# The last chunk's outer column sums on VectorE, and the last but one chunk's store from SyncE

## The chip, the cores and the metric

The kernel runs on one core of one Trainium2 chip, as a single launch. The metric is device time in microseconds. A core has five engines with an in-order instruction queue each: TensorE (PE; its weight loads are listed as PEld), VectorE (DVE), ScalarE (ACT), GpSimd (POOL) and SyncE (SP). DMAs can be issued from several of them; here SP issues plain DMAs, and GpSimd issues plain ones and those that add what they read to what is at the destination (accumulating DMAs). An instruction that waits on a semaphore holds everything behind it on its own queue.

## The reference

The input is four images of 256 channels and 56 x 56 points, in f32. Four layers follow, each of the form x + layer(group_norm(x)) with 32 groups:

```python
# layer 0 and 2: involution, a 7x7 kernel computed per point (16 groups of 16 channels)
h    = einsum('bchw,oc->bohw', x, reduce_w)      # 256 -> 64; layer 2: batch norm, relu
kern = einsum('bchw,oc->bohw', h, span_w)        # 64 -> 49 * 16
out  = (kern * patches(x)).sum(over the 49 taps) # layer 2: batch norm, relu
# layer 1: two 3x3 convolutions over 256 channels
h = relu(bn(conv3x3(x, w1)))
h = bn(conv3x3(h, w2))
out = relu(x + h)
# layer 3: gates from 2-d Fourier transforms of the image
out = x * sigmoid(real fft mean @ W.T + b) + x * spatial_factor
```

The change lies in layer 1, in its second convolution. Here `x` inside the layer is the normalized input, so that the result of the layer is xin + relu(xnorm + bn(conv(h))), where xin is the input before the norm.

## The kernel before

`involution_layer` does layer 0, `conv_layer` layer 1, and `involution_layer` again layers 2 and 3. Images that aren't in SBUF lie in DRAM, in one tensor for each layer, image and half of the channels (128 of 256).

**Tiling of the convolution.** The layer has twelve chunks (`n_chunks = 3 * B`): each image is cut into three bands of rows (`C2_ROWS`: 16, 20 and 20 rows). For each chunk there is a `conv1` and a `conv2`, in the order conv1(i), conv2(i - 1); at the end come conv1(11), conv2(10), conv2(11). So conv2(11), "the last chunk", follows conv2(10), "the last but one", with no conv1 between. Along a row the convolution is done by a transform of six positions for four outputs: `transform` (L1439 to 1455) makes six transformed inputs `v`, TensorE multiplies each with transformed weights, and VectorE combines the six products into four outputs.

**Six positions in order.** `KS = (1, 2, 3, 4, 0, 5)`. In conv2, positions 1, 2, 3 and 5 are `unfiltered` (L1525): three rows of weights for two halves of input channels, with 280 columns. Positions 4 and 0 are filtered (`filtered_product`, L1540): the rows are transformed as well, and the product needs sums and differences of neighbouring rows of `v`. `inner_columns` (L1491 and L1492) makes two of them on VectorE. `outer_columns` makes the other two, v of a row minus v two rows below, in one of two ways:

```python
if (conv, i) == (1, 1):
    tt(t[:, at], v[:, at], v[:, below], ALU.subtract)        # L1505, VectorE
else:
    nc.scalar.mul(t[:, at], v[:, below], -1.0)               # L1507, ScalarE
    nc.gpsimd.dma_start(t[:, at], v[:, at], accum_op=ALU.add)  # L1508, GpSimd
```

Here `tt` is VectorE's tensor_tensor. For the last chunk the destination `t` is free room in the weights of the first convolution (`u1_sb`; the profile shows it as u_sb). A filtered product runs its 16 inner matmuls first and its 16 outer matmuls behind them. ScalarE copies the first inner result (L1549), VectorE makes sum and difference with the second (L1550, L1551), and adds the outer results (L1553). The combination of outputs follows (L1723 to L1734), and after the product of position 5, one half of the output channels at a time (`co` 0 and 1), L1741 and L1742.

**The end of a chunk.** For the last two chunks the residual comes in by `load_residual` (L1392, issued by SP) into one of two buffers that alternate (`new_xr`), and ScalarE scales it (`residual`, L1633). In `joined`, VectorE adds the result of the convolution (L1670). The last chunk then takes VectorE (L1675) and a store from SP (L1676). The last but one uses `added`: a Relu on ScalarE (L1684), an accumulating DMA on GpSimd that adds xin (L1685), and a store on GpSimd (L1686). Its statistics for the next layer's norm are taken on VectorE from the same buffer (`stats`, L1704), in the course of conv2(11). The residual of the last chunk is loaded into the same two buffers, so each load waits for the store and the statistics of the half that it replaces.

**Order of the work.** The order on each engine is the order in which the program calls are made (`in_order`). Twelve lists `after[0]` to `after[11]` hold steps that are run at two points of each of six positions: in `conv2`, `after[2 * n_s]` comes between the two halves of a product (in a filtered product, between L1551 and L1553) and `after[2 * n_s + 1]` behind the combination. For conv2(11): `inner_columns` and the outer sums of position 4 are in `after[2]`, those of position 0 in `after[3]`; the statistics of chunk 10 are in `after[3]` and `after[4]` (co 0) and `after[6]` and `after[7]` (co 1), and the residual loads behind them in `after[4]` and `after[7]`. `added` goes through the list `late_x`: for co 0 it is run at once, for co 1 it is left for `after[0]` of the next piece of work (L1804), that is, for conv2(11) behind the first half of its first product.

Of the kernel before, what the change touches and what calls it, by code (L numbers as in the profile page):

```python
# [73 lines left out]
def net_kernel(  # L74
# [19 lines left out]
    nc = tc.nc  # L94
# [1089 lines left out]
    def conv_layer(xin, xout, st, ahead):  # L1184
        with ExitStack() as es:
# [40 lines left out]
            def new_xr():  # L1226
                n_xr[0] += 1
                at = (n_xr[0] - 1) % 2 * NX
                return room["xr"][:, at : at + NX]
# [9 lines left out]
            def new_outer():  # L1239

                n_v2[1] += 1
                at = (n_v2[1] - 1) % 5
                return room["v2"][:, at * NY : (at + 1) * NY]
# [136 lines left out]
            n_chunks = 3 * B  # L1380
# [86 lines left out]
            def input2(i):  # L1467
                v = v_of[2, i] = v_sb[i == n_chunks - 1]
                p0, p1 = C2_ROWS[i % 3 - 1]
                yield from transform(  # L1470
                    v, ph2, i % 2 * PH_ROWS, (19, 20, 19)[i % 3], v_of.get((2, i - 1)), p1 - p0, known_rows(i, 3)
                )

            def rows_of(conv, i):

                y0, y1 = (C1_ROWS if conv == 1 else C2_ROWS)[i % 3]
                return y1 - y0
# [16 lines left out]
            def outer_columns(conv, i, k):  # L1494

                n = rows_of(conv, i)
                v = v_of[conv, i][:, VP[k]].rearrange("p r t -> p (r t)")
                if (conv, i) == (2, n_chunks - 1):
                    t = u1_sb[:, FILTERED2.index(k)].rearrange("p y k n -> p (y k n)")[:, 2 * NX : 2 * NX + NY]
                else:  # L1500
                    t = new_outer()
                at = slice(0, n * NB * WT)
                below = slice(2 * NB * WT, (n + 2) * NB * WT)
                if (conv, i) == (1, 1):
                    tt(t[:, at], v[:, at], v[:, below], ALU.subtract)  # L1505
                else:
                    nc.scalar.mul(t[:, at], v[:, below], -1.0)  # L1507
                    nc.gpsimd.dma_start(t[:, at], v[:, at], accum_op=ALU.add)  # L1508
                t = t.rearrange("p (r e n) -> p e r n", e=2, n=NB * WT)
                v2_of[conv, i, k, 1] = [t[:, e] for e in range(2)]  # L1510


            def run_all(items):
                while items:
                    items.pop(0)()
# [97 lines left out]
            def conv2(i, after, sums, tail):  # L1613
# [4 lines left out]
                bb = i // 3  # L1618
# [22 lines left out]
                def joined(co):  # L1641

                    y = room["h"][:, : 4 * NY].rearrange("p (j n) -> p j n", j=4)[:, :, co * m : (co + 1) * m]
                    if summed:
                        x, at = new_xr(), slice(y0 * W, y1 * W)
                        xr_of[i, co] = x
                        x = x[:, : n * W]
                        s, t = (raw[:, co : co + 1] for raw in raw_of[bb])
                        by = rstd[:, co : co + 1]

                        def leaves():
                            nc.scalar.activation(x.rearrange("p (q j) -> p j q", j=4), y, AF.Identity, bias=t, scale=s)
                            nc.gpsimd.dma_start(x, xin[bb][co][:, at], accum_op=ALU.add)

                        if co == 0:
                            leaves()
                        else:
                            late_r[0].append(leaves)
                        k = 5 + 2 * co
                        late_r[k].append(lambda: nc.scalar.activation(x, x, AF.Relu, scale=by))  # L1660
                        late_r[k + 1].append(lambda: nc.gpsimd.dma_start(x, xin[bb][co][:, at], accum_op=ALU.add))
                        k = 10 + 2 * co
                        late_r[k + 1].append(lambda: nc.sync.dma_start(xout[bb][co][:, at], x))
                        if bb < B - 1:
                            st = sums[co][:, i % 3]
                            late_r[k].append(lambda: mean_of(st, x))
                            late_r[k + 4].append(lambda: spread_of(st, x))
                        return
                    rj = results[co].rearrange("p (j q) -> p j q", j=4)
                    stt(rj, y, s2_6[:, co : co + 1], rj, ALU.mult, ALU.add)  # L1670
                    x = xr_of[i, co][:, : n * W]
                    xj = x.rearrange("p (q j) -> p j q", j=4)
                    at = slice(y0 * W, y1 * W)
                    if i == n_chunks - 1:
                        stt(xj, rj, 0.0, xj, ALU.max, ALU.add)  # L1675
                        nc.sync.dma_start(xout[bb][co][:, at], x)  # L1676
                    else:
                        late_x.append(lambda: added(x, xj, rj, co, at))
                        if co == 0:
                            run_all(late_x)  # L1680

                def added(x, xj, rj, co, at):

                    nc.scalar.activation(xj, rj, AF.Relu)  # L1684
                    nc.gpsimd.dma_start(x, xin[bb][co][:, at], accum_op=ALU.add)  # L1685
                    nc.gpsimd.dma_start(xout[bb][co][:, at], x)  # L1686

                def mean_of(st, x):

                    nc.gpsimd.memset(st[:, 0:1], float(n * W))  # L1690
                    nc.scalar.activation(x, x, AF.Identity, accum_out=st[:, 1:2])
                    nc.scalar.mul(st[:, 1:2], st[:, 1:2], 1.0 / (n * W))

                def spread_of(st, x):

                    c = small.tile([P, 1], F32, name="c")
                    nc.scalar.mul(c, st[:, 1:2], -1.0)
                    nc.scalar.activation(x, x, AF.Square, bias=c, accum_out=st[:, 2:3])
# [38 lines left out]
                for co in range(NB):  # L1737
                    at = slice(co * m, (co + 1) * m)
                    ps = one_bank()[:, :m]
                    unfiltered(ps, u2_sb, v, 5, co, n)  # L1740
                    stt(q[:, at], q[:, at], -3.0, ps, ALU.mult, ALU.add)  # L1741
                    stt(q[:, at], t[:, at], 4.0, q[:, at], ALU.mult, ALU.add)  # L1742
                    joined(co)
                    run_all(after[10 + co])
# [8 lines left out]
            def columns_at(after, inner, outer, conv, i):  # L1753
                for at, ks in zip(inner, ((1, 2), (3, 4))):
                    after[at].append(lambda ks=ks: inner_columns(conv, i, *ks))
                for at, k in outer:
                    after[at].append(lambda k=k: outer_columns(conv, i, k))
# [6 lines left out]
            for i in range(1, n_chunks):  # L1764
                order += [(1, i), (2, i - 1)]
            order.append((2, n_chunks - 1))
            late_v, late_x, late_r = None, [], [[] for _ in range(24)]
            sums_of = {}


# [27 lines left out]
            for s, (conv, i) in enumerate(order):  # L1798
                after = [[] for _ in range(12)]
# [1 line left out]
                    after[5].append(step(g))  # L1801
                    after[11].append(step(g))
                nxt = order[s + 1] if s + 1 < len(order) else None
                after[0] += late_x  # L1804
                late_x.clear()
                for items in after:
                    items += late_r.pop(0)
                    late_r.append([])
                if conv == 1:
# [3 lines left out]
                    if i > 0:  # L1813
                        after[0].append(lambda i=i: (inner_columns(1, i, 0, 5), outer_columns(1, i, 0)))
                        if i > 1:
                            after[2].append(lambda i=i: outer_columns(1, i, 5))
                    if nxt[0] == 2:
                        j = nxt[1]
                        late_v = input2(j)
# [25 lines left out]
                else:  # L1845
# [10 lines left out]
                    if late_v is not None:  # L1856
                        place(after, late_v, (0, 0, 1, 1))
                        late_v = None
# [44 lines left out]
    def begin_last():  # L1903
# [3 lines left out]
        norm_weights(2, 0)  # L1907

    pending = conv_layer(src[1], src[2], st, begin_last)
    involution_layer(2, src[2], src[3], red2, span2, sb2, blocks, pending=pending)  # L1910

# [64 lines left out]
```

## Time and profile before

| | us |
|---|---|
| median of three runs | 1714.48 |
| the three runs | 1714.85, 1708.15, 1714.48 |
| the profiled execution | 1717.23 |
| its span, first to last instruction | 1715.5 |
| TensorE busy (share of the span) | 1632.9 (95%) |
| VectorE busy | 1333.8 (78%) |
| ScalarE busy | 1000.9 (58%) |
| GpSimd busy | 498.2 (29%) |
| mean granted TensorE clock | 0.979 |

Times in the profile count from the start of the span. In it, conv2(10) ends near 1126 us and conv2(11) near 1173 us. A line of the timeline or of the chain gives the start, the length, and the engine with its line in the code; outputs stand left of the arrow, inputs right. In brackets is the time for which the engine was idle before, and what released it. A wait of an instruction for several semaphores is put down to the one that came last.

### The profile page before, as it was taken

The page shows a single profiled execution, that of the slowest core. Times are in us where ns is not written, and L with a number is a line of the kernel's source. Part 1 is how long each engine was busy: PE and PEld are TensorE (multiplying, and loading weights), DVE is VectorE, ACT ScalarE, POOL GpSimd, SP SyncE. Part 2 cuts the span into 40 slices and gives each one's busy share as a digit, 9 for nine tenths or more (in the row PEclk, how much of TensorE's full clock was granted, in tenths as well). Part 3 has the DMA queues.
Part 4 walks back from the last instruction along what each step waited for, and adds up shares of the span by engine and source line. Part 5 has one row for each costly group of instructions (what it writes and reads, how often), then busy time and mean ns, then how long its engine had stood idle before and what let it go on. Part 6 is the DMA issues. An engine that isn't in the chain of part 4 may idle for free.

```text
span 1715.5 us, 57009 instructions
## 1 busy us (share of the span) xinstructions
PE 1632.9 (95%) x24488; PEld 1466.1 (85%) x24488; DVE 1333.8 (78%) x2439; ACT 1000.9 (58%) x2192; POOL 498.2 (29%) x711
## 2 busy tenths in 40 slices
PE   6999999999989999999999999988999999899988
PEld 4998998988987889899999889976988888788876
DVE  2687787777759998999889899947777778778775
ACT  1655556456545565565666456435667567577654
POOL 2124223322433222212212212110000572572571
PEclk9999999999999999999999999999999999999996
DMA  2354445433759666566766556644444765764762
GB/s 90 114 184 138 147 147 185 154 127 104 238 139 281 112 129 106 121 129 138 148 132 113 109 122 128 142 132 147 129 139 162 207 215 184 218 210 140 204 169 98
DMA packets 92490, 258.63 MB, mean 151 GB/s; under 512 B 14837, under 2 KB 37374, under 8 KB 88526
## 3 DMA queue, kind: packets, MB, share of 16 engines
q1 hardware_dynamic: 57438, 163.33, 29.9%
q0 software_dynamic: 33760, 90.37, 24.8%
q8 instruction: 194, 3.18, 0.8%
q10 hardware_dynamic: 1040, 1.26, 0.3%
q14 instruction: 58, 0.48, 0.1%
HBM read 95.07 MB, written 49.15 MB: 84 GB/s over the span
## 4 chain that ended last, share of the span: by engine, by line
PE 64%; DVE 15%; DMA 7%; issue 5%; ACT 3%; SPq 2%; POOL 2%; ACTq 0%; POOLq 0%; DVEq 0%
PE mm L1540 17%; PE ps L594 15%; PE ps L636 13%; PE mm L1525 11%; DVE kt L612 5%; DMA xw<-xw 4%; PE ps L408 3%; DVE un L656 3%; DMA u_sb<-in_wc_dram 2%; PE ps L470 1%; SPq L426 1%; SPq L427 1%; DVE st L1106 1%; ACT hp L489 1%; ACT xw L420 1%
## 5 line engine op out<-in xcount | busy, mean ns | idle before, releaser
L636 PE MATMUL ps<-kt,xw 126*32 126x48 f32 (+1 forms) x12544 | 381.7, 236 | 24.1 <-DMA xw<-xw 11.3
L636 PEld LDWEIGHTS ps<-kt,xw 126*32 126x32 f32 (+1 forms) x12544 | 343.0, 122 | 69.7 <-issue 44.0
L594 PE MATMUL ps<-hp,z_sb 64*126 64x133 f32 x6144 | 384.3, 279 | 9.0 <-DVE kt L612 4.9
L594 PEld LDWEIGHTS ps<-hp,z_sb 64*126 64x126 f32 x6144 | 364.4, 185 | 25.0 <-DVE kt L612 6.9
L612 DVE TENSOR_TENSOR kt<-ps,zb_sb 126x798 f32<-126x798 f32 x352 | 332.9, 980 | 59.3 <-PE ps L594 47.9
L605 ACT ACTIVATE kt<-ps,zb_sb 126x133 f32<-126x133 f32 x960 | 281.0, 442 | 107.3 <-PE ps L594 107.3
L1525 PE MATMUL mm<-v,u_sb 128*128 128x280 f32 (+2 forms) x1320 | 295.1, 383 | 1.7 <-DVE xs L1551 1.0
L1525 PEld LDWEIGHTS mm<-v,u_sb 128*128 128x128 f32 x1320 | 247.5, 189 | 41.8 <-issue 1.6
L1540 PE MATMUL mm<-xs,u_sb 128*128 128x126 f32 (+2 forms) x1392 | 175.9, 279 | 0.3 <-DVE xs L1551 0.3
L656 DVE SCALAR_TENSOR_TENSOR un<-ps,s,un 128x240 f32<-128x240 f32 x224 | 102.5, 457 | 89.0 <-ACT un L651 83.7
L1540 PEld LDWEIGHTS mm<-xs,u_sb 128*128 128x128 f32 x1392 | 168.5, 193 | 0.5 <-issue 0.5
L656 DVE SCALAR_TENSOR_TENSOR un<-ps,par_sb,un 128x240 f32<-128x240 f32 x224 | 97.6, 456 | 81.8 <-ACT un L649 77.9
L1508 POOL DMA_DIRECT2D xs<-v x82 | 75.2, 1006 | 285.3 <-ACT xs L1507 233.9
L661 POOL TENSOR_TENSOR xs<-un,xs 128x240 f32<-128x240 f32 x112 | 72.2, 665 | 216.3 <-DVE un L656 216.3
L420 ACT COPY xw<-ps 126x896 f32<-126x896 f32 x112 | 101.4, 906 | 39.0 <-PE ps L408 21.3
L649 ACT ACTIVATE un<-ps,par_sb 128x240 f32<-128x240 f32 x112 | 50.3, 449 | 119.1 <-PE ps L636 112.8
L151 POOL TENSOR_TENSOR norm_sb<-norm_sb,mhalf 128x1 f32<-128x1 f32 x32 | 19.8, 642 | 342.5 <-DVE norm_sb L150 342.5
L651 ACT ACTIVATE un<-ps,bn_t,s 128x240 f32<-128x240 f32 x112 | 60.1, 538 | 94.2 <-PE ps L636 86.0
L408 PE MATMUL ps<-ident_sb,strip_sb 128*126 128x128 f32 x784 | 110.6, 281 | 3.9 <-ACT hp L489 1.6
L408 PEld LDWEIGHTS ps<-ident_sb,strip_sb 128*126 128x126 f32 x784 | 84.0, 141 | 15.0 <-POOL strip_sb L393 4.6
L1411 ACT ACTIVATE ph<-xs,norm_sb 128x266 f32<-128x266 f32 (+2 forms) x96 | 80.4, 862 | 9.0 <-DMA xs<-x 7.3
L1540 PE MATMUL mm<-v_sb,u_sb 128*128 128x140 f32 (+2 forms) x536 | 73.5, 280 | 3.5 <-DVE xs L1553 3.0
(303 smaller groups left out, 2272.7 us busy)
## 6 DMA issues: line engine op xcount, KB each, us to landing
xw<-xw SPq DMA_DIRECT2D x224, 252.0 KB
xw<-xw SPq DMA_DIRECT2D x224, 126.0 KB
xs<-x POOLq DMA_DIRECT2D x26, 560.0 KB, 5.9
x<-xs POOLq DMA_DIRECT2D x8, 1568.0 KB, 7.8
xs<-x SPq DMA_DIRECT2D x8, 1568.0 KB
xs<-v POOLq DMA_DIRECT2D x42, 252.0 KB, 4.3
xs<-in_x_dram SPq DMA_DIRECT2D x6, 1568.0 KB
x<-xs SPq DMA_DIRECT2D x6, 1568.0 KB
```

The source lines that it names most:

```text
L408: nc.tensor.transpose(ps[:Q, k * P : (k + 1) * P], flat[:, k * Q : (k + 1) * Q], ident_sb)
L420: nc.scalar.copy(xw[:, :NSB, :], ps[:Q, : NSB * P].rearrange("q (n c) -> q n c", n=NSB))
L594: nc.tensor.matmul(ps[:Q, i, k * NT : (k + 1) * NT], z_sb[i * R : (i + 1) * R, cb * GB // 2 + gp, z0 : z0 + Q], hp[i * R : (i + 1) * R, py ...
L605: nc.scalar.activation(kt[:, g0 + i, pb, :, k], ps[:Q, i, k * NT : (k + 1) * NT], AF.Identity, bias=zb_sb[:, cb * GB + g0 + i, p0 + k : p0 ...
L612: nc.vector.tensor_tensor(kt[:, g0 : g0 + 2, pb], ps[:Q, :, : PB * NT].rearrange("q i (k t) -> q i t k", k=PB), zb_sb[:, cb * GB + g0 : cb ...
L636: nc.tensor.matmul(v[m * j : m * j + m, i, :, k * TP : (k + 1) * TP], xw[:, window(ty), m * j : m * j + m], kt[:, ng * j : ng * j + ng, :, ...
L656: nc.vector.scalar_tensor_tensor(part, o[e], s, part, ALU.mult, ALU.add)
L661: nc.gpsimd.tensor_tensor(dst, u, dst, ALU.add)
L1411: nc.scalar.activation(dst, xr[:, j], AF.Identity, bias=t, scale=s)
L1508: nc.gpsimd.dma_start(t[:, at], v[:, at], accum_op=ALU.add)
L1525: nc.tensor.matmul(ps, *position(u, v, ci, dy, k, co, n), start=(j == 0), stop=(j == NB * 3 - 1))
L1540: nc.tensor.matmul(ps[:, bank, co * m : (co + 1) * m], u[ci][:, co * P : (co + 1) * P], v2[:, : n // 2, ci * WT : (ci + 1) * WT], start=(c ...
```

## The change

There are two edits. The outer column sums of conv2's last chunk are made by one VectorE subtraction for each of positions 4 and 0, where ScalarE's multiply and GpSimd's accumulating DMA made them. In the last but one chunk `added` is called for both halves of the output channels directly in `joined`, without `late_x`, and its store is issued by SP where GpSimd issued it. The Relu and the accumulating DMA stay where they were, on ScalarE and GpSimd.

```diff
@@ outer_columns
-                if (conv, i) == (1, 1):
+                if (conv, i) in ((1, 1), (2, n_chunks - 1)):
                     tt(t[:, at], v[:, at], v[:, below], ALU.subtract)
                 else:
                     nc.scalar.mul(t[:, at], v[:, below], -1.0)
@@ joined
                     else:
-                        late_x.append(lambda: added(x, xj, rj, co, at))
-                        if co == 0:
-                            run_all(late_x)
+                        added(x, xj, rj, co, at)
 
                 def added(x, xj, rj, co, at):
 
                     nc.scalar.activation(xj, rj, AF.Relu)
                     nc.gpsimd.dma_start(x, xin[bb][co][:, at], accum_op=ALU.add)
-                    nc.gpsimd.dma_start(xout[bb][co][:, at], x)
+                    nc.sync.dma_start(xout[bb][co][:, at], x)
@@ conv_layer
-            late_v, late_x, late_r = None, [], [[] for _ in range(24)]
+            late_v, late_r = None, [[] for _ in range(24)]
@@ the loop over the order
-                after[0] += late_x
-                late_x.clear()
```

## The prediction

> **What bounds the kernel now.** I read the page, then the timeline at the end of the convolution layer (1100 to 1180 us), where both edits lie, then the waits, the chain and the stretches there. The page's TensorE is 95% busy over a span of 1715.5 us, so a gain has to come from a place where TensorE stands still. The waits of 1100 to 1180 us (who waited for whom: total us, times, longest) show one:
>
> ```profile
> PE mm L1540 <- DMA u_sb<-v: 7.6, 1, 7.6
> DVE xs L1553 <- PE mm L1540: 8.5, 1, 8.5
> POOL x L1686 <- DMA xs<-x: 11.5, 2, 6.2
> ACT u_sb L1633 <- DMA xs<-x: 18.4, 3, 9.4
> ```
>
> TensorE stops for 7.6 us for the outer column sums of the last chunk (u_sb), and VectorE then stops 8.5 us for TensorE. The chain (start us, us, what) says why the sums are late:
>
> ```profile
> 1140.04 0.86 POOL xs L1685
> 1140.90 6.22 issue
> 1147.12 0.04 POOLq L1508
> 1147.16 0.50 POOL x L1686
> 1147.66 0.01 issue
> 1147.67 4.11 DMA u_sb<-v
> 1151.78 0.14 issue
> 1151.91 4.09 PE mm L1540 x16
> ```
>
> GpSimd issues the residual's accumulation for the second channel half of chunk 10 (L1685), then stands 6.22 us before the store of the same half (L1686), which needs it landed, and only then issues the two accumulations that make the outer sums (L1508). Those land 4.1 us later. The timeline (start, us, engine and line; in brackets the idle time before and its releaser):
>
> ```profile
> 1133.34 0.88 POOL L1685 DMA_DIRECT2D xs<-x  x1 [28.17 <-ACT xs L1684]
> 1135.44 1.22 ACT L1507 ACTIVATE u_sb<-v 128x560 f32<-128x560 f32 x2
> 1136.85 0.74 DVE L1723 TENSOR_TENSOR hp<-hp,mm 128x560 f32<-128x560 f32 x1 [3.25 <-ACT u_sb L1507]
> 1144.79 0.45 DVE L1550 TENSOR_TENSOR xs<-xs,mm 128x280 f32<-128x280 f32 x1 [4.04 <-ACT xs L1549]
> 1148.28 2.36 ACT L1633 ACTIVATE u_sb<-xs,shift,norm_sb 128x1120 f32<-128x1120 f32 x1 [3.52 <-DMA xs<-x]
> 1156.02 0.74 DVE L1553 TENSOR_TENSOR xs<-xs,mm 128x560 f32<-128x560 f32 x1 [8.53 <-PE mm L1540]
> ```
>
> ScalarE's half of the sums was done by 1136.7; eleven more us went by at GpSimd. From 1156.02 VectorE works almost without a gap to the end of the layer (L1675 at 1172.70), and the next layer begins behind it. Here VectorE's chain sets the time, and what releases L1553 is the lever.
>
> **What the Trainium skill says.** "DMA: Bandwidth & Descriptors", section "SWDGE vs HWDGE vs iDMA": an accumulating DMA must come from GpSimd, a plain one may come from SP. So the stores can move and L1685 cannot; the trace has it on GpSimd. Same page, "Queues, rings and completion order": each DMA engine takes turns between queue rows, so a store from SP shares the engines with GpSimd's accumulation in place of standing ahead of it. The load of 1142.65, beside an accumulation, landed after 5.6 us; that of 1160.5, alone, after 3.75. "VectorE: DVE Perf Modes", "The perf-mode tier table": tensor_tensor in f32 runs at one element a cycle; the trace's 560 columns take 0.734 us (L1505, five of them). "TensorE: Matmul & The Clock Gate", Part 1: a window of about 3.4 us idle halves the clock; the trace grants 0.50 from 1152 to 1156, after the stall.
>
> **The change, part by part.**
>
> *Outer sums on VectorE.* Gone: two ScalarE multiplies (2 x 0.655) and two GpSimd DMAs with 4.1 us to landing. Added: two subtractions, 2 x 0.734 = 1.47 us on VectorE. The first follows L1492 at 1133.6, and VectorE then idles to 1136.85 (3.25 us): hidden. The second follows the first statistics of chunk 10 (after 1139.4) and has the 4.04 us ahead of L1550 at 1144.79: hidden too. Without that cover they would cost 1.47. Both are ready ahead of their products, so TensorE goes on at 1144.33 and ends the 16 outer products at about 1146.4 (2.07 us, as the same group at 1113.45), in place of 1155.98 (4.07 at the low clock).
>
> *Store by SP, second half at once.* ScalarE's order stays: the two Relus of L1684 already run back to back, since nothing of ScalarE lies between. On GpSimd, L1685 of the second half waits no more for the first half's landing (1139.4) and store: it is issued when its Relu ends, at 1135.1, 4.9 us earlier. The first accumulation keeps the engines busy from about 1134.9 to 1138.5 (3.7 us; seen as landed at 1139.4). The second, behind it in the same queue, ends 3.7 us later at 1142.3 and is seen at 1143.1, in place of 1147.1.
> On SP come two stores, ahead of the load of the last chunk's residual (L1392), and SP now waits for each accumulation. Behind those waits stands only this load: the block loads of the next layer were issued by 1119.8. First store: issued 1139.5, alone 3.1 us to landing, plus 0.9 to 1.4 beside the accumulation (half of 5.6 - 3.75 is 0.9): 1143.5 to 1144.0. Second store: issued at 1143.1, 0.32 for the issue. The load needs the first store landed: issued 1143.6 to 1144.0, landing 3.75 + 0.9 later, 1148.25 to 1148.9. Before it was 1148.25. I take 1148.5.
>
> *Where the stall goes.* From L1553 at 1156.02 to L1550 of the next product at 1160.37 VectorE's work is 4.35 us (L1553, L1728 to L1731, two statistics). Now L1553 can start at 1146.45: L1550 at 1150.8, if nothing else is late. But its ScalarE copy stands behind the residual's scaling (L1633), which starts when the load lands: 1148.5 + 2.36 + 0.40 and 0.09 between = 1151.35. That load is late next and decides. The second residual load follows the statistics at 1150.9 and lands by 1154.7, scaled by 1157.1, wanted at 1169.08 - 9.0 = 1160.1: hidden. TensorE's products of position 5 end near 1156.5, before they are wanted. From L1550 to L1675's end are 12.33 us, unchanged.
> Sum: 1160.37 - 1151.35 = 9.0 us off everything that follows. Bounds: 9.57 if the load is early (VectorE's own 1150.8), 8.6 at a landing of 1148.9; ends for the unknown sharing of the engines: 1147 to 1151.
>
> **The numbers.** The profiled execution took 1717.23 us, 1.73 around its span: 1717.23 - 9.0 = 1708.2, span 1706.5. It lies 2.75 above the median of 1714.48; the same saving gives 1705.5.
>
> **Rivals.**
> *Late load.* The store of the second half holds the load on SP while both halves share the engines, and the 7.6 us go in part to L1633's wait. For it: ScalarE already waits 3.5 us for this load. Against: the accumulation starts 4.9 us earlier. If it lands at 1150.5, L1550 is at 1153.35: 7.0 us, 1707.5; at 1152.5, 1709.5.
> *More than the stall.* The stretches grant 0.76 and 0.81 of the clock from 1168 to 1176 and 0.61 from 1184 to 1188. If they owe this to the stall, up to 4 x (0.24 + 0.19 + 0.39) = 3.3 us come on top: 12.3, 1702.2. Against: from 1164 to 1168 and from 1176 to 1184 TensorE is busy half the time, which the change leaves.
> *Slower.* SP's order turns round: if two accumulations in flight take twice their 6.2 us each (landing 1136.0 + 12.4 = 1148.4) and the load behind the store twice its 5.6 (issued 1148.8, landing 1160.0), L1550 is at 1162.9, 2.5 us later than before: 1717.0. This decides from a landing at 1157.5, and costs 0.5% from 1166. Against: in the accumulations' middle the engines are busy already (0.99 from 1136 to 1138), so two take the sum, not more.
> *The change does nothing new* if the outer sums were not the last wait of TensorE there: the 16 products started 0.13 us after the sums' landing, so they were.
>
> **How the numbers follow.** Forecast 0.60 (its own range 1703 to 1708 with the scatter), late load 0.24, clock 0.09, slower 0.07. The three runs of before spread over 6.7 us, and about 0.5%, 8.6 us, is what a measurement can tell from no change: the forecast lies just beyond it. Faster by over that: 0.58 of the forecast's 0.60 and the clock's 0.09, 0.67. Within: 0.24 + 0.02 + 0.01 of the slower case, 0.27. Slower: 0.06. The range, 1700 to 1711, holds the first three with a scatter of 2 to 3 us for a median, and leaves the slower case out.
>
> **What would show it.** Right: no wait of L1540 for u_sb; two more L1505 of 0.73 us near 1133.6 and 1140; L1685's two issues 1.8 us apart; L1550 of the last product near 1151.4; L1675 ending near 1163.7; L1633's first wait for its load in the place of the stall. Wrong: a load that lands after 1150, an accumulation seen after 1145, or statistics (L1704) that hold the second subtraction beyond 1144.8. Clock losses after 1164 that differ from before would move the total without touching these steps.

## The result, and the profile after

The changed kernel takes 1703.01 us (median of 12 runs, 1699.88 to 1708.69), beside 1714.42 us for the kernel before in the same measurement (12 runs, 1708.15 to 1717.83). The ratio is 0.9935, with a 95% interval of 0.9921 to 0.995: 0.65% faster, 0.5 to 0.8. In a second measurement beside two later experiments it was 0.993 (0.9904 to 0.9956). Forecast was 1705.5, or 0.9948.

The profiled execution took 1704.8 us, with a span of 1703.0 us.

In the changed file the lines behind L1676 stand two lower: the accumulation L1685 is now L1683, the store L1686 is L1684, L1704 is L1702, L1723 is L1721. Two of the waits of the changed kernel from 1100 to 1180 us:

```profile
ACT u_sb L1633 <- DMA xs<-x: 16.4, 3, 9.6
DVE xs L1550 <- ACT xs L1549: 3.3, 1, 3.3
```

TensorE's wait for u_sb (7.6 us before), VectorE's wait for TensorE at L1553 (8.5) and GpSimd's two waits ahead of the store (11.5) are no longer in the list. SP waits for the accumulations instead, and behind it stands only the load of the residual. The timeline of the same place (start, us, engine and line; in brackets the idle time before and its releaser):

```profile
1123.53 17.23 PE L1525 MATMUL mm<-v,u_sb 128*128 128x280 f32 x72
...
1131.81 0.88 POOL L1683 DMA_DIRECT2D xs<-x  x1 [28.31 <-ACT xs L1682]
1131.98 0.73 DVE L1505 TENSOR_TENSOR u_sb<-v 128x560 f32<-128x560 f32 x1
...
1133.85 0.87 POOL L1683 DMA_DIRECT2D xs<-x  x1 [1.16 <-ACT xs L1682]
1135.19 0.74 DVE L1721 TENSOR_TENSOR hp<-hp,mm 128x560 f32<-128x560 f32 x1 [2.47 <-issue]
...
1137.67 3.01 SPq L1684 DMA_DIRECT2D x<-xs  x2
1138.19 0.72 DVE L1505 TENSOR_TENSOR u_sb<-v 128x560 f32<-128x560 f32 x1
...
1141.80 7.58 SPq L1392 DMA_DIRECT2D xs<-x  x2
...
1142.50 2.07 PE L1540 MATMUL mm<-u_sb 128*128 128x140 f32 x16
...
1144.60 0.74 DVE L1553 TENSOR_TENSOR xs<-xs,mm 128x560 f32<-128x560 f32 x1
...
1145.73 2.50 ACT L1633 ACTIVATE u_sb<-xs,shift,norm_sb 128x1120 f32<-128x1120 f32 x1 [2.64 <-DMA xs<-x]
...
1148.94 0.43 DVE L1550 TENSOR_TENSOR xs<-xs,mm 128x280 f32<-128x280 f32 x1
...
1159.08 2.20 DVE L1675 SCALAR_TENSOR_TENSOR xs<-u_sb,xs 128x1120 f32<-128x1120 f32 x1
```

The two subtractions (L1505) lie in VectorE's idle time. The accumulations are issued 2.0 us apart and not 6.7. TensorE's outer products have no wait ahead of them and take 2.07 us, at a granted clock of 1.00 from 1140 to 1144 (4.07 us before, at 0.50), and L1550 of position 0 has no idle time before it.

Executions of either kernel differ by some us in parts that the change does not touch. The last chunk can be read free of that, since its first matmul (the x72 group above) stands ahead of both edits. In the kernel before, that group, two steps of VectorE, and the first work of TensorE behind the next layer's preparation (the first L594) are:

```profile
1125.19 17.23 PE L1525 MATMUL mm<-v,u_sb 128*128 128x280 f32 x72
...
1160.37 0.43 DVE L1550 TENSOR_TENSOR xs<-xs,mm 128x280 f32<-128x280 f32 x1
...
1170.50 2.19 DVE L1675 SCALAR_TENSOR_TENSOR xs<-u_sb,xs 128x1120 f32<-128x1120 f32 x1
...
1182.44 7.40 PE L594 MATMUL ps<-hp,z_sb 64*126 64x133 f32 x96 [2.01 <-ACT hp L489]
```

In the changed kernel the first L594 starts at 1171.01. Counted from the start of that group:

| us from the group's start to | before | after | difference |
|---|---|---|---|
| L1553 of position 4 | 30.83 | 21.07 | 9.76 |
| L1550 of position 0 | 35.18 | 25.41 | 9.77 |
| the end of the last L1675 | 47.50 | 37.75 | 9.75 |
| the first L594 | 57.25 | 47.48 | 9.77 |

The whole saving arises at one place, is there in full at L1553, and nothing of it is given back up to the first L594. A second profiled execution of the changed kernel gives 47.47 in place of 47.48. The two spans differ by 12.5 us: 1.66 ahead of the group, 9.77 in the stretch, 1.07 behind the first L594. Over all thirteen profiled executions of this study the group starts between 1123.5 and 1128.0 us, and the time behind the first L594 is 526.2 to 535.0 us, in no order that follows the edits; the 1.66 and 1.07 are within that scatter. One place of it is seen in the traces: the first 96 matmuls of L594 take 6.04 us in the two executions that grant them a mean clock of 1.00, 7.16 to 7.40 at 0.80 to 0.77, and 8.64 in the one that grants 0.65.

### The profile page after: what moved, and what is told of

The parts are those of the page before. It is cut to its first block, busy times and chain, and to the rows that moved or that the text cites. A ratio compares the mean times of both kernels' runs of the same rounds, so it can differ in the third digit from the quotient of the medians.

```text
span 1703.0 us, 56999 instructions
## 1 busy us (share of the span) xinstructions
PE 1632.3 (96%) x24488; PEld 1464.7 (86%) x24488; DVE 1335.5 (78%) x2441; ACT 998.8 (59%) x2190; POOL 496.6 (29%) x707
## 3 DMA queue, kind: packets, MB, share of 16 engines
q10 hardware_dynamic: 1040, 1.26, 0.3%
## 4 chain that ended last, share of the span: by engine, by line
PE 68%; DVE 17%; DMA 5%; issue 5%; ACT 4%; POOL 1%; SPq 1%; ACTq 0%; POOLq 0%; DVEq 0%
PE mm L1540 17%; PE ps L594 14%; PE mm L1525 14%; PE ps L636 13%; DVE kt L612 6%; DMA xw<-xw 4%; DVE un L656 3%; PE ps L408 3%; PE ps L470 2%; DVE st L1106 1%; ACT hp L489 1%; SPq L426 1%; ACT xw L420 1%; PE ps L719 1%; PE ps L948 1%
## 5 line engine op out<-in xcount | busy, mean ns | idle before, releaser
L594 PE MATMUL ps<-hp,z_sb 64*126 64x133 f32 x6144 | 383.9, 279 | 9.0 <-DVE kt L612 5.8
L594 PEld LDWEIGHTS ps<-hp,z_sb 64*126 64x126 f32 x6144 | 363.7, 185 | 25.3 <-DVE kt L612 8.0
L1652 ACT ACTIVATE xs<-hp,raw,raw 128x1120 f32<-128x1120 f32 (+1 forms) x20 | 45.7, 2285 | 51.0 <-DVE hp L1740 51.0
```

The source lines that it names most:

```text
L594: nc.tensor.matmul(ps[:Q, i, k * NT : (k + 1) * NT], z_sb[i * R : (i + 1) * R, cb * GB // 2 + gp, z0 : z0 + Q], hp[i * R : (i + 1) * R, py ...
```

## The experiments

The theory: what was worth time is that GpSimd's queue held the outer sums behind a store's wait. Each edit takes them out of there alone, so the two gains overlap. Rivals: the edits share the gain; the early second half is what matters; the sums' own DMA time is on the path. "Stretch" below is the time from the start of the last chunk's first matmul group to the first L594, 57.25 before and 47.48 after. It is read from one profiled execution of each run; the ratio is of the whole time.

### Only the outer sums on VectorE

```diff
-                if (conv, i) == (1, 1):
+                if (conv, i) in ((1, 1), (2, n_chunks - 1)):
```

> Only the outer sums on VectorE; the last but one chunk keeps its late second half and its store from GpSimd. Theory: the stall came from GpSimd's queue, and each edit alone takes the outer sums out of it, so the two gains overlap. TensorE no longer waits for u_sb, but the second half's accumulation is still issued at 1140.0 and lands at 1147.1 (times of before), the statistics that need it end at 1147.8, VectorE's addition L1553 follows them in place of 1156.0, and L1550 of position 0 comes 4.35 us later at 1152.1: 8.2 us gained (7.5 to 9), ratio 0.995. Rival (the edits share the gain between them): 4 to 6 us. In the trace: L1553 released by the statistics' wait for the accumulation, of 1 to 2 us.

The ratio to before is 0.9953 (0.9935 to 0.997); the stretch is 48.27 us (1123.67 to 1171.94), so 8.98 gained. Timeline:

```profile
1145.00 0.63 DVE L1704 BATCH_NORM_STATS2 st_c<-xs 128x6 f32<-128x448 f32 x1 [0.81 <-DMA xs<-x]
1145.27 0.56 POOL L1686 DMA_DIRECT2D x<-xs  x1 [6.06 <-DMA xs<-x]
1145.55 0.72 DVE L1553 TENSOR_TENSOR xs<-xs,mm 128x560 f32<-128x560 f32 x1
```

GpSimd still stands 6 us ahead of the store, and it costs no more than 0.8 us of the stretch, because nothing urgent is behind it. The next wait is the one named: L1553 stands behind statistics that need the late accumulation. It is shorter than expected (0.81 us): VectorE goes on 0.3 us before GpSimd does, and these statistics start 0.35 us earlier in the stretch than before (21.33 and 21.68 us after the group's start). The rival of a shared gain falls.

### Only the second half at once and the stores by SP

```diff
-                if (conv, i) in ((1, 1), (2, n_chunks - 1)):
+                if (conv, i) == (1, 1):
```

(the changed kernel, with this line as before)

> Only the second half at once and the stores by SP; the outer sums stay with ScalarE and GpSimd. Theory: the sums' two accumulations (L1508) are issued at about 1136 and 1137 (times of before), right behind the two accumulations of the residual, not at 1147.7, and land near 1144 and 1146, before or just when TensorE wants them (1144.3 and 1148.6). They delay the load of the last residual by about 2 us: L1550 near 1152, 8 us gained (7 to 9), ratio 0.995. Rival (the 4 us from issue to landing of such a sum is itself on the path): TensorE still waits 3 us or more for u_sb, gain 4 to 6 us.

Ratio 0.9954 (0.9941 to 0.9967); stretch 51.25 (1124.66 to 1175.91), so 6.0 us gained: less than expected. Timeline:

```profile
1135.74 1.76 POOL L1508 DMA_DIRECT2D u_sb<-v  x2 [0.16 <-issue]
...
1138.69 3.06 SPq L1684 DMA_DIRECT2D x<-xs  x2
...
1143.63 2.07 PE L1540 MATMUL mm<-u_sb 128*128 128x140 f32 x16
...
1145.92 4.59 SPq L1392 DMA_DIRECT2D xs<-x  x2
...
1151.11 2.39 ACT L1633 ACTIVATE u_sb<-xs,shift,norm_sb 128x1120 f32<-128x1120 f32 x1 [6.88 <-DMA xs<-x]
```

The sums do land in time: TensorE waits for u_sb no more, and the rival that put their DMA time on the path falls. What takes the wait's place is the load of the last residual. It needs the first store landed, and that store, issued at 1138.69, lets the load go only at 1145.92, 7.2 us later, where in the changed kernel it is 4.1 (1137.67 to 1141.80). In both the store runs beside the second half's accumulation; here the sums' two accumulations run beside it as well. So L1633 starts 4.25 us later in the stretch than in the changed kernel (26.45 and 22.20 us after the group's start): 3.0 us because the load is issued later, and 1.26 because it takes longer itself (5.19 us from its issue to L1633, 3.93 in the changed kernel). L1550 comes 3.75 us later.

### Only the engine of the store

```diff
-                    nc.gpsimd.dma_start(xout[bb][co][:, at], x)
+                    nc.sync.dma_start(xout[bb][co][:, at], x)
```

> The kernel before with one word changed: the store of the last but one chunk is issued by SP and not by GpSimd; the late second half and the outer sums on ScalarE and GpSimd stay. Theory: the wait of this store on GpSimd's queue is the whole cause, so this is worth the same as the stores together with the second half at once, 8 us (7 to 9), ratio 0.995. Rival (the early call of the second half matters): clearly less than that run, by 3 us or more.

Ratio 0.996 (0.9944 to 0.9976); stretch 50.33 (1127.53 to 1177.86), 6.92 us gained, just below the expected range. Timeline:

```profile
1153.04 2.41 ACT L1633 ACTIVATE u_sb<-xs,shift,norm_sb 128x1120 f32<-128x1120 f32 x1 [5.94 <-DMA xs<-x]
...
1155.76 0.45 DVE L1550 TENSOR_TENSOR xs<-xs,mm 128x280 f32<-128x280 f32 x1 [2.57 <-ACT xs L1549]
```

It is no worse than the run with the second half called at once (6.0), so that call adds nothing, and again the load of the residual is what is late (L1633 25.51 us after the group's start). Of the 0.9 us between the two runs, the load itself accounts for nearly all: L1633 starts 4.31 us after its issue here and 5.19 there. Why it does was not tested.

### Only the early call

```diff
-                    nc.sync.dma_start(xout[bb][co][:, at], x)
+                    nc.gpsimd.dma_start(xout[bb][co][:, at], x)
```

(the run "only the second half at once and the stores by SP", with its store back on GpSimd)

> Only the second half's Relu, accumulation and store called at once and not in the next chunk; store still from GpSimd, outer sums still on ScalarE and GpSimd. Theory: nothing, since GpSimd's order stays the same (accumulate, store, accumulate, store, sums): ratio 1.000 within 0.002, TensorE's wait for u_sb still 7 to 8 us. Rival (the early call matters): 3 us or more faster.

Ratio 1.0004 (0.9986 to 1.0022); stretch 57.18. Three of its waits:

```profile
POOL x L1684 <- DMA xs<-x: 11.5, 2, 6.2
DVE xs L1553 <- PE mm L1540: 8.5, 1, 8.5
PE mm L1540 <- DMA u_sb<-v: 7.5, 1, 7.5
```

All three waits of the kernel before are back. No effect of the removal of `late_x` on the time is seen; the store's engine and the sums' engine carry it all.

### The subtractions twice

```diff
-                    tt(t[:, at], v[:, at], v[:, below], ALU.subtract)
+                    for _ in range(1 if conv == 1 else 2):
+                        tt(t[:, at], v[:, at], v[:, below], ALU.subtract)
```

> The changed kernel with each of the last chunk's two subtractions run twice, 1.47 us more on VectorE. Theory: the two places are covered by VectorE's idle time (2.47 us ahead of L1721 and 3.26 us ahead of L1550 in the changed kernel), so the stretch from the first matmul of the last chunk to the end of L1675 stays at 37.8 us (within 0.2), and those two idle times shrink to about 1.7 and 2.5. Rival (VectorE's order is on the path there already): 38.5 to 39.3 us.

This kernel was run once. The time from the group's start to the end of L1675 is 37.76 us (37.75 in the changed kernel). The line numbers are one higher behind L1505. The idle times have shrunk and not gone:

```profile
1136.53 0.74 DVE L1722 TENSOR_TENSOR hp<-hp,mm 128x560 f32<-128x560 f32 x1 [1.95 <-PE mm L1526]
...
1144.45 0.45 DVE L1551 TENSOR_TENSOR xs<-xs,mm 128x280 f32<-128x280 f32 x1 [2.66 <-ACT xs L1550]
```

So the added VectorE work is hidden, and was so even twice over.

### The load of the residual later

```diff
-                nc.sync.dma_start(xr[:, : (y1 - y0) * W], xin[i // 3][co][:, y0 * W : y1 * W])
+                for _ in range(2 if (i, co) == (n_chunks - 1, 0) else 1):
+                    nc.sync.dma_start(xr[:, : (y1 - y0) * W], xin[i // 3][co][:, y0 * W : y1 * W])
```

> The changed kernel with the load of the last residual's first half done twice, the second into the same place and so behind the first's landing. Theory: the load is next in line behind VectorE's own work, with 0.4 us to spare; the second landing is 3.75 us later, so L1633 starts about 3.8 us later, L1549 behind it, L1550 about 3.4 us later, and the stretch to the end of L1675 goes from 37.8 to 41.2 us; ratio to before 0.9960. Rival (the load has room to spare, VectorE alone decides): below 38.5 us.

Ratio 0.997 (0.9951 to 0.999); the stretch to the end of L1675 is 41.46 us, to the first L594 51.20, 3.7 us more than in the changed kernel. Line numbers one higher behind L1392:

```profile
1152.80 2.40 ACT L1634 ACTIVATE u_sb<-xs,shift,norm_sb 128x1120 f32<-128x1120 f32 x1 [6.85 <-DMA xs<-x]
...
1155.51 0.45 DVE L1551 TENSOR_TENSOR xs<-xs,mm 128x280 f32<-128x280 f32 x1 [3.62 <-ACT xs L1550]
```

ScalarE's scaling starts 4.2 us later than in the changed kernel (26.41 and 22.20 us after the group's start), VectorE's L1550 3.7: the load has 0.5 us to spare in the changed kernel. It is next in line, and the timelines of the two runs with the sums on GpSimd show the same chain: there it cost them part of their gain.

### The first half of the last chunk by ScalarE and GpSimd

The theory says that VectorE's chain ends the layer. Then L1675 of the first half (2.17 us) can be taken from it, by finishing that half as chunk 10 is finished.

```diff
-                    if i == n_chunks - 1:
+                    if i == n_chunks - 1 and co == 1:
                         stt(xj, rj, 0.0, xj, ALU.max, ALU.add)
```

> The changed kernel with the last chunk's first half finished as the last but one chunk is: Relu on ScalarE, accumulation on GpSimd, store by SP, in place of VectorE's L1675 (2.17 us). Theory: VectorE's chain to the end of the layer sets the time, ScalarE is idle there, so 2.2 us come off: stretch to the end of L1675 35.6 us. But SP now waits for the accumulation (landing about 5.3 us after its issue) ahead of the next layer's loads of z_sb, which go out 1 us later at least than VectorE's gain would let them, so TensorE's first L594 may gain less, 0 to 2.2 us. Ratio to before 0.992. Rival (something else than VectorE ends the layer): the stretch stays at 37.8 us.

> As the run with the first half finished by ScalarE and GpSimd, but its store is put with the statistics that the next layer runs behind its first products, so that SP waits for nothing. Theory: the whole 2.2 us: stretch to the end of L1675 35.6 us, to the first L594 45.3 us in place of 47.5; ratio to before 0.992, 0.0013 below the changed kernel's. Rival (SP's wait cost nothing): the same as with the early store.

The second run differs by its store:

```diff
-                    nc.sync.dma_start(xout[bb][co][:, at], x)
+                    store = lambda: nc.sync.dma_start(xout[bb][co][:, at], x)
+                    if i == n_chunks - 1:
+                        tail.append([store])
+                    else:
+                        store()
```

The stretch to the end of L1675 is 35.62 us in both, to the first L594 45.27 and 45.28: 2.2 us less than in the changed kernel. VectorE's chain did end the layer. SP's wait for the accumulation, which the first of the two has (its store goes out at 1164.10, issued behind the accumulation of 1158.26), costs nothing up to there. But the ratios to before are 0.9942 (0.9924 to 0.9959) and 0.9944 (0.993 to 0.9959), no better than the changed kernel's 0.9935. So all three were run again side by side.

> The changed kernel as it is, beside the two that follow. Ratio to before 0.9935 to 0.9945: the stretch from the first matmul of the last chunk to the first L594 is 9.8 us shorter than before (47.5 in place of 57.3), and what the whole time shows beyond that is scatter of the layers before and behind, in which the span behind the first L594 went from 526 to 533 us over the executions so far. If instead the change also gains elsewhere, the ratio stays at or below 0.9930.

> As before with the first half of the last chunk finished by ScalarE and GpSimd, once more beside the changed kernel. If the 2.2 us that the stretch loses are kept, the ratio to before lies 0.0013 below the changed kernel's of the same call; if they are given back later (TensorE's granted clock is lower in the first L594 group, 8.1 us in place of 7.4), the two are equal within 0.0005.

> As the run before it with the store behind the next layer's first statistics. The same two outcomes: 0.0013 below the changed kernel's ratio if the 2.2 us are kept, equal if given back.

The ratios were 0.993 (0.9904 to 0.9956) for the changed kernel, 0.994 (0.9917 to 0.9963) and 0.993 (0.9904 to 0.9955). The intervals are wider than the 0.0013 in question, so whether the whole kernel gains by the 2.2 us stays open. So does the question in the first expectation: 0.993 lies at the edge of what a gain elsewhere would show, and the interval takes in both outcomes. Part of the 2.2 us is seen to go back. In the repeated run of the changed kernel and in the repeated run of the first variant the timelines show, one after the other:

```profile
1126.53 17.23 PE L1525 MATMUL mm<-v,u_sb 128*128 128x280 f32 x72
...
1174.00 7.73 PE L594 MATMUL ps<-hp,z_sb 64*126 64x133 f32 x96 [1.35 <-ACT hp L489]
...
1183.60 17.34 PE L594 MATMUL ps<-hp,z_sb 64*126 64x133 f32 x288 [0.47 <-DVE kt L612]
```

```profile
1126.84 17.23 PE L1525 MATMUL mm<-v,u_sb 128*128 128x280 f32 x72
...
1172.12 8.11 PE L594 MATMUL ps<-hp,z_sb 64*126 64x133 f32 x96 [1.08 <-ACT hp L489]
...
1182.16 17.33 PE L594 MATMUL ps<-hp,z_sb 64*126 64x133 f32 x288 [0.47 <-DVE kt L612]
```

The first 96 of these matmuls take 8.11 us in place of 7.73 (7.16 in the first execution of the changed kernel), and the next group starts 55.32 us after the beginning in place of 57.07 (56.51). Of the 2.2 us, 1.2 to 1.75 are left there. The clock granted to the first 96 was 0.70, and 0.74 and 0.80 in the two executions of the changed kernel. All four executions of the two variants show 0.69 or 0.70 and 8.07 to 8.18 us, so the loss goes with the granted clock. What sets this clock was not tested.

## Why the prediction was right, and where it was off

The time, 1703.0, lies in the range of 1700 to 1711 and 2.5 us below the forecast of 1705.5. The likeliest case, the stall gone with 8.6 to 9.6 us of gain, is the one that came: the stretch shows 9.77 us. Of the 2.5 us, 0.8 lie in the stretch. The rest has no explanation in the prediction or in the traces.

- **Place and cause: right.** GpSimd's wait ahead of the store held the outer sums. Moving either of the two things out of that queue ends TensorE's wait, and calling the second half early without that does nothing.
- **Outer sums at no cost: right**, shown by running them twice.
- **The second accumulation earlier: right, size off.** Forecast 1143.1 in place of 1147.1. Measured, the second store goes out at 1140.36 (1137.67 + 3.01 - 0.32), or 1142.0 with the 1.66 us by which this execution is ahead: 5 us earlier, not 4.
- **The residual load decides: wrong by a little.** This is the step that failed. I put the load's issue at 1143.6 to 1144.0 and its landing 3.75 + 0.9 us later, and L1550 behind it, at 1151.35. It was issued at 1141.80 (1143.46 with the 1.66 us), and L1633 started 3.93 us after that: the 0.9 for sharing the engines was too much by 0.7, and the issue came 0.1 to 0.5 us sooner. With 0.5 us to spare the load is hidden, and VectorE's own order sets L1550: 25.41 us after the group's start, where the forecast had 26.16 and its bound for an early load 25.61. The last 0.2 is TensorE's: its outer products started 18.97 us after the group's start, where the forecast had 19.14. So 9.77 us were gained and not 9.0.
- **The "late load" rival** has the right mechanism, but with both edits it does not come to bear. It is what the two runs with the sums on GpSimd show, at 6.0 and 6.9 us.
- **The "more than the stall" rival: not seen.** The shift at the first L594 (9.77) is that at L1675 (9.75). The granted clock right behind the chunk is not better: 0.60 and 0.55 from 1156 to 1164, where before had 0.76 and 0.81 from 1168 to 1176. In the first L594 group it is 0.80 (0.77 before).
- **The "slower" rival: not seen.** The two accumulations in flight together took 7.7 us (from 1132.69, the end of the first issue, to 1140.36); one after the other they had taken 5.2 and 6.2.
- **What the prediction left out:** it gave each edit its own account and did not say that they overlap. The sums on VectorE alone give 8.98 of the 9.77 us. The store on SP adds 0.8 to that, though alone it gives 6 to 6.9. And the 0.8 is shown only up to the first L594. The next group of L594 starts 55.95 us after the beginning with the sums alone (clock 1.00 in the first L594 group), and 56.51 and 57.07 in the two executions of the changed kernel (0.80 and 0.74). The intervals of the ratios overlap as well (0.9935 to 0.997, and 0.9921 to 0.995), so that the second edit gains anything in the whole time is not shown.

The median's 11.4 us are 1.6 more than the stretch explains. That lies inside the interval (8.6 to 13.5 us), and no place in the traces was found for it. In the other runs with an interval, too, the gain by the ratio differs from that of the stretch, by up to 2.4 us either way.

## What to carry to other kernels

A wait costs what stands behind it on its queue: the 6 us that GpSimd stood ahead of a store cost 9 us when it held the sums that TensorE needed next, and 0.8 at most when those were made elsewhere. When two edits take the same thing out of one queue, don't add their gains: ask what each gives alone, and which wait is next (here a load, 0.5 us behind). And where executions scatter by several us, count from a matmul group ahead of the edit: two executions of the changed kernel agreed to 0.01 us in this stretch, where the interval of twelve runs was 2.5 us wide to either side. What is gained in the stretch can still be lost behind it, as with the 2.2 us of the last experiment.

## What the runs showed that I had not expected

A store from SP took longer the more accumulations from GpSimd ran beside it. The 560 KB store of the first half let the waiting load go 3.2 us after its issue when it stood on GpSimd's queue ahead of the next accumulation (1139.44 to 1142.65), 4.1 us beside one accumulation, and 7.2 and 7.0 us beside one and the two of the outer sums. In all the runs with SP the second half's store is under way for the last part of this time as well (in the changed kernel from 1140.36), and its share was not measured apart. The store was not simply kept behind the accumulations: in the changed kernel it let the load go 1.4 us after the second accumulation had landed (1141.80 and 1140.36), less than the 3.2 us that it took in the kernel before. That is in line with what the Trainium skill says in "DMA: Bandwidth & Descriptors", section "Queues, rings and completion order", that each DMA engine takes turns between queue rows; the prediction used it for one accumulation, and my expectation for the runs with the sums on GpSimd, 2 us for the two more, was too small.
